# A third neighbour from SBUF, part of a fourth by SyncE, and VectorE's register loads moved: the item stage of a recommender kernel

## Chip, cores and metric

The kernel runs on one core of a Trainium2 chip. The metric is the device time of one execution in microseconds, as a median over runs. One further execution was recorded by the hardware profiler; durations of single instructions come from that one.

## What is computed

There are 50001 items. Each has two embeddings of 32 numbers (E_in, E_out), an embedding of 64 numbers, and 32 neighbours. For each item and each of the two tables, the scores against the 32 neighbours pass through a softmax, and the neighbours' rows are summed with these weights. This makes a table of 128 numbers per item. Then, for 16384 users with a history of 100 items and a target each, rows of that table are fetched, multiplied with the target's row, sent through a layer of 128 units, and weighted.

```python
def _neighbor_attn(E, near_full):
    V = E[near_full]
    scores = jnp.einsum('nd,nkd->nk', E, V) / jnp.sqrt(jnp.float32(GEO_HALF))
    w = jax.nn.softmax(scores, axis=-1)
    return jnp.einsum('nk,nkd->nd', w, V)
...
a_sus = _neighbor_attn(E_in, near_full)
a_inf = _neighbor_attn(E_out, near_full)
hist_bi = jnp.concatenate([a_sus[history], a_inf[history]], axis=-1)
h = jnp.concatenate([E_hist[history], hist_bi], axis=-1)
x = h * t[:, None, :]
z = jax.nn.relu(jnp.einsum('bld,hd->blh', x, W1) + b1)
scores = jnp.einsum('blh,h->bl', z, W2[0])
```

## The kernel before

The kernel has two stages, one after the other. The **item stage** fills the table in DRAM; the **user stage** gathers from it (12800 indirect DMAs at L438, 128 rows each) and is not touched by the change.

The item stage works on blocks of 128 items, one item per partition. NITER x NSUB = 23 x 17 = 391 blocks; `load(it)` (L128 to L163) brings indices, own embeddings and rows for 17 blocks at a time by SyncE. For a block s the tile v holds the 32 neighbours of each of the 128 items, 64 numbers (both tables) per neighbour, so 256 bytes. It is filled in two ways:

- `gather(s)` (L198) issues one indirect DMA per neighbour on GpSimd (L215): 128 rows of 256 bytes, one to each partition. With NAUX = 2 it does so for 30 of the 32 neighbours. A path on which SyncE fetches one neighbour row by row (L206 to L213) stands in the code, but SPNUM = 0 leaves it unused.
- The last NAUX neighbours come out of SBUF. The whole two-table embedding is held transposed in geoT, two items to a column (`transposed`, L165, done once at the start out of 66 loads st at L171). `columns(s, a, i0)` (L222) loads 32 column addresses into registers of one engine (L189) and issues 32 small copies, geoT column to g column (L229). `turn` (L231) transposes g back on TensorE, `even` (L238, ScalarE) and `odd_half` (L245, VectorE, a predicated copy) put the right half of the column into v. AUX says which engine copies which 32 columns: "AAAA" is four groups on ScalarE (A), "DDDD" four on VectorE (D).

After that VectorE multiplies v with the item's own row (prod, L258), sums to scores (L268), takes the largest (L272, L273); ScalarE makes the exponents (L281); VectorE weights the neighbours (L294, once per table), sums (L309) and scales (L310); ScalarE copies the result into the second table's row (`finish`, L317), and every 17 blocks writes both tables.

The order is written out by hand: the stage runs under a manual schedule for TensorE, ScalarE, VectorE and SyncE, so each engine executes in the order of the code. In turn s of the loop at L337, GpSimd gathers block s, block s-1 is scored, block s-2 weighted, block s-3 finished. Eight pieces of work (L343) alternate with the groups of copies for block s (L353 to L359), which are dealt out evenly over the eight. v has five buffers, g two, wv and prod one. DMAs issued by SyncE and ScalarE share eight completion semaphores in rotation, and the next DMA on one waits for the one before.

Of the kernel before, what the change touches and what calls it, by code (L numbers as in the profile page):

```python
# [31 lines left out]
NSUB = 17  # L32
# [2 lines left out]

AUX = ("AAAA", "DDDD",)
NAUX = len(AUX)
SPNUM, SPDEN = 0, 1  # L40
ENGINE = {"A": E.Activation, "D": E.DVE}
NREG = 32
PAIRS = ROWS // 2
# [11 lines left out]
def kernel(  # L55
# [57 lines left out]
    with (  # L113
# [11 lines left out]
        its = {}  # L125
        subs = {}
# [71 lines left out]
        def gather(s):  # L198
            it, j = divmod(s, NSUB)
            nidx = its[it][0]  # L200
            v = n_v.tile([P, K, 2, G], F32, name="v")
            g = [n_g.tile([P, P], F32, name=f"g{a}") for a in range(NAUX)]
            subs[s] = {"v": v, "g": g}
            k1 = K - NAUX - 1
            by_sp = s * SPNUM % SPDEN < SPNUM
            if by_sp:  # L206
                for i0 in range(0, P, NREG):
                    vals = registers(s, 0, E.SP, i0, 0, (ITEMS - 1) * 8 * G)
                    for i in range(NREG):
                        nc.sync.dma_start(  # L210
                            v[i0 + i : i0 + i + 1, k1].rearrange("p t d -> p (t d)").bitcast(U8),
                            egeo_b[:, ds(vals[i], 8 * G)],
                        )  # L213
            for k in range(k1 if by_sp else k1 + 1):
                nc.gpsimd.indirect_dma_start(  # L215
                    out=v[:, k].rearrange("p t d -> p (t d)"),
                    out_offset=None,
                    in_=egeo,
                    in_offset=bass.IndirectOffsetOnAxis(ap=nidx[:, j, k : k + 1], axis=0),
                )  # L220

        def columns(s, a, i0):  # L222

            e = AUX[a][i0 // NREG]
            vals = registers(s, a + 1, ENGINE[e], i0, geoT_at, geoT_at + 4 * (PAIRS - 1))
            g = subs[s]["g"][a].bitcast(U8)
            copy = nc.scalar.copy if e == "A" else nc.vector.tensor_copy
            for i in range(i0, i0 + NREG):
                copy(g[:, 4 * i : 4 * i + 4], geoT_b[:, ds(vals[i - i0] - geoT_at, 4)])  # L229

        def turn(s):  # L231
            back = n_pt.tile([P, 4, P], F32, name="pt")
            for a in range(NAUX):
                nc.tensor.transpose(back[:, a, :], subs[s]["g"][a], ident)  # L234
            subs[s]["back"] = back
            subs[s]["aux"] = subs[s]["v"][:, K - NAUX : K].rearrange("p k t d -> p k (t d)")

        def even(s):  # L238
            it, j = divmod(s, NSUB)
            nc.scalar.copy(subs[s]["aux"], subs[s]["back"][:, 0:NAUX, 0 : 2 * G])  # L240
            own_ps = n_ps.tile([P, 1, 2 * G], F32, name="own_ps")
            nc.scalar.copy(own_ps[:, 0, :], its[it][1][:, j, :])
            subs[s]["own"] = own_ps

        def odd_half(s):  # L245
            it, j = divmod(s, NSUB)
            nc.vector.copy_predicated(
                subs[s]["aux"],
                its[it][4][:, j, :]
                .rearrange("p (a o) -> p a o", o=1)  # L250
                .to_broadcast([P, NAUX, 2 * G]),
                subs[s]["back"][:, 0:NAUX, 2 * G : 4 * G],
            )

        def products(s):
            v = subs[s]["v"]
            prod = n_p.tile([P, K, 2, G], F32, name="prod")
            nc.vector.tensor_tensor(  # L258
                prod.rearrange("p k t d -> p k (t d)"),
                v.rearrange("p k t d -> p k (t d)"),  # L260
                subs[s]["own"].to_broadcast([P, K, 2 * G]),
                ALU.mult,
            )
            subs[s]["prod"] = prod

        def scores(s):
            sc = n_s.tile([P, 2, K], F32, name="sc")
            nc.vector.tensor_reduce(  # L268
                sc.rearrange("p t k -> p k t"), subs[s]["prod"], AX.X, ALU.add
            )  # L270
            top = n_s.tile([P, 2], F32, name="top")
            nc.vector.tensor_reduce(top, sc, AX.X, ALU.max)  # L272
            nc.vector.tensor_scalar(top, top, -scale, None, ALU.mult)  # L273
            subs[s]["sc"] = (sc, top)

        def exponents(s):
            sc, top = subs[s]["sc"]
            ex = n_ps.tile([P, 2, K], F32, name="ex")
            tot = n_s.tile([P, 2, 1], F32, name="tot")
            for t in range(2):  # L280
                nc.scalar.activation(  # L281
                    ex[:, t, :],
                    sc[:, t, :],
                    AF.Exp,
                    bias=top[:, t : t + 1],
                    scale=scale,
                    accum_out=tot[:, t, :],
                )
            subs[s]["ex"] = (ex, tot)

        def weighted(s, t):
            if t == 0:
                subs[s]["wv"] = n_p.tile([P, 2, G, K], F32, name="wv")
            nc.vector.tensor_tensor(  # L294
                subs[s]["wv"][:, t].rearrange("p d k -> p k d"),
                subs[s]["v"][:, :, t, :],
                subs[s]["ex"][0][:, t, :]
                .rearrange("p (k o) -> p k o", o=1)
                .to_broadcast([P, K, G]),
                ALU.mult,  # L300
            )

        def attend(s):
            it, j = divmod(s, NSUB)
            row = its[it][2]
            tot = subs[s]["ex"][1]
            nc.vector.reciprocal(tot, tot)
            att = n_s.tile([P, 2, G], F32, name="att")
            nc.vector.tensor_reduce(att, subs[s]["wv"], AX.X, ALU.add)  # L309
            nc.vector.tensor_tensor(  # L310
                row[:, j, DE:D].rearrange("p (t d) -> p t d", t=2),
                att,
                tot.to_broadcast([P, 2, G]),
                ALU.mult,
            )

        def finish(s):  # L317
            it, j = divmod(s, NSUB)
            _, _, row, trow, _, _ = its[it]
            for t in range(2):  # L320
                nc.scalar.copy(
                    trow[:, j, t * G : (t + 1) * G], row[:, j, D - (t + 1) * G : D - t * G]
                )
            if j == NSUB - 1:
                nc.scalar.dma_start(table_v[it], row)
                nc.scalar.dma_start(ttab_v[it][:, :, DE:D], trow)
                del its[it]
            del subs[s]

        NT = NITER * NSUB  # L330
# [3 lines left out]
        blocks = [(a, i0) for a in range(NAUX) for i0 in range(0, P, NREG)]  # L334
        acts = [(a, i0) for a, i0 in blocks if AUX[a][i0 // NREG] == "A"]
        dves = [(a, i0) for a, i0 in blocks if AUX[a][i0 // NREG] == "D"]
        for s in range(NT + 3):  # L337
            if s < NT:
                if s % NSUB == NSUB // 2 and s // NSUB + 1 < NITER:
                    load(s // NSUB + 1)  # L340
                gather(s)
            one, two, three = (0 <= s - d < NT for d in (1, 2, 3))
            work = [  # L343
                lambda: one and turn(s - 1),
                lambda: (two and weighted(s - 2, 0), one and even(s - 1)),
                lambda: two and weighted(s - 2, 1),
                lambda: one and (odd_half(s - 1), products(s - 1)),
                lambda: one and scores(s - 1),
                lambda: two and attend(s - 2),
                lambda: three and finish(s - 3),  # L350
                lambda: one and exponents(s - 1),
            ]
            for w in range(len(work)):  # L353
                work[w]()
                if s < NT:
                    for blocks in (acts, dves):
                        n = len(blocks)
                        for c in blocks[-(-w * n // 8) : -(-(w + 1) * n // 8)]:
                            columns(s, *c)  # L359


    num = const.tile([P, UC], F32, name="num")
# [8 lines left out]
    with (  # L371
# [125 lines left out]
        for s in range(len(groups) + 2):  # L497
            if s < len(groups):
                c, g = groups[s]
# [12 lines left out]
    with (  # L512
# [12 lines left out]
        s = f_s.tile([P, 1], F32, name="s")  # L525
# [72 lines left out]
```

## Time and profile before

| | |
|---|---|
| median of 3 runs | 30856.08 us (30855.88 to 30856.29) |
| the profiled execution | 30865.45 us, of it 30863.6 us span |
| GpSimd busy | 23284.3 us, 75% |
| VectorE busy | 12128.8 us, 39% |
| ScalarE busy | 7843.2 us, 25% |
| gathers of the item stage (L215) | 11730, 944 ns each |
| gathers of the user stage (L438) | 12800, 944 ns each |
| copies at L229 | 50048 on ScalarE, 50048 on VectorE |
| granted TensorE clock, mean | 0.802 |

In the profile, POOL is GpSimd, DVE is VectorE, ACT is ScalarE, SP is SyncE, PE is TensorE; a q behind the name means that the engine's sequencer issues and the engine itself stays idle. A row of the groups gives the line, the operation, out<-in, the count, then busy time in us and mean ns of one, then the idle time of the engine just before these instructions and what ended it. "issue" is idle time that no recorded event of another engine ended. A row of the waits gives who waited for whom: total us, times, longest. A row of the timeline gives start, duration, and in brackets the idle time before. Loads of registers do not count as busy; they show as idle time of the engine. The small copies at L229 overlap each other, so a group of 32 is much shorter than 32 times the mean.

### The profile page before, as it was taken

To read this page: it belongs to the slowest core of one execution; us is meant where nothing else is said; L and a number is where in the kernel's file an instruction comes from. 1 tells how busy PE (TensorE), PEld (TensorE's weight loads), DVE (VectorE), ACT (ScalarE), POOL (GpSimd) and SP (SyncE) were. 2 spreads that over 40 slices of the span, in tenths; PEclk is the share of its full clock that TensorE was granted. 3 is DMA by queue.
4 is the path that set the end of the run, shared out by engine and by line. 5 is a ranking of instruction groups with operands and counts; after the bars stand their busy time and mean duration, and the time that the engine had idled before them with its cause. 6 is when DMAs were issued, how large, how long until landed. Compare 5 with 4: busy or idle time off the path is not lost.

```text
span 30863.6 us, 246685 instructions
## 1 busy us (share of the span) xinstructions
PE 13340.6 (43%) x45932; PEld 7630.5 (25%) x45932; DVE 12128.8 (39%) x58485; ACT 7843.2 (25%) x56963; POOL 23284.3 (75%) x24664
## 2 busy tenths in 40 slices
PE   0000000000000000000778778877877877887787
PEld 0000000000000000000444444444444544454444
DVE  5555555555555555555222222222222222222222
ACT  4333333333333333333111111111111111111111
POOL 7777777777777777777777777777777777777777
PEclk9999999999999999999665666666566566656656
DMA  2111111111111111111222222222222222222221
GB/s 67 31 31 31 32 34 31 31 31 32 34 31 31 31 35 31 31 31 29 54 53 54 54 53 54 53 53 53 54 53 54 53 54 53 53 53 54 53 54 52
DMA packets 966199, 1351.82 MB, mean 44 GB/s; under 512 B 548416, under 2 KB 561280, under 8 KB 961696
## 3 DMA queue, kind: packets, MB, share of 16 engines
q0 software_dynamic: 789056, 1233.20, 17.1%
q10 hardware_dynamic: 103920, 51.31, 0.6%
q1 hardware_dynamic: 71664, 51.54, 0.6%
q14 instruction: 1192, 9.76, 0.1%
q8 instruction: 367, 6.01, 0.1%
HBM read 1295.95 MB, written 51.30 MB: 44 GB/s over the span
## 4 chain that ended last, share of the span: by engine, by line
POOL 56%; issue 23%; DMA 12%; PE 7%; DVE 1%; another core or an unknown queue 0%; ACT 0%; POOLq 0%; SPq 0%; ACTq 0%; DVEq 0%
POOL v L215 33%; POOL h L438 23%; DMA h<-table,hidx 10%; PE z_ps L473 3%; DMA v<-in_egeo_dram,nidx 2%; PE score L482 2%; PE hT_ps L453 2%; DVE xT L455 1%; DVE hsum L458 0%; DMA st<-in_egeo_dram 0%; PE pt L180 0%; POOL t L400 0%; POOLq L438 0%; ACT g L229 0%
## 5 line engine op out<-in xcount | busy, mean ns | idle before, releaser
L438 POOL DMA_INDIRECT h<-table,hidx x12800 | 12084.6, 944 | 3899.7 <-issue 3451.0
L215 POOL DMA_INDIRECT v<-in_egeo_dram,nidx x11730 | 11078.2, 944 | 3599.4 <-issue 3484.2
L453 PE MATMUL hT_ps<-ident,h 128*128 128x128 f32 x12800 | 5070.5, 414 | 3207.2 <-DMA h<-table,hidx 3025.5
L455 DVE TENSOR_TENSOR xT<-hT_ps,tT 128x1024 f32<-128x1024 f32 (+1 forms) x1664 | 1968.4, 1183 | 10942.7 <-PE hT_ps L453 10942.5
L234 PE MATMUL pt<-ident,g 128*128 128x128 f32 x782 | 363.9, 471 | 13297.0 <-DVE g L229 8118.8
L473 PE MATMUL z_ps<-xT,w1T 128*128 128x512 f32 x6400 | 5799.9, 1007 | 26.6 <-DVE xT L455 26.3
L229 ACT COPY g<-geoT 128x4 uint8 x50048 | 4919.0, 189 | 2153.7 <-issue 2152.4
L474 ACT ACTIVATE z<-z_ps,b_sb 128x512 f32<-128x512 f32 x3200 | 2201.1, 688 | 12756.3 <-PE z_ps L473 12748.7
L229 DVE COPY g<-geoT 128x4 uint8 x50048 | 3885.9, 194 | 2268.1 <-issue 2149.5
L453 PEld LDWEIGHTS hT_ps<-ident,h 128*128 128x128 f32 x12800 | 2439.0, 194 | 8517.2 <-DMA h<-table,hidx 7853.9
L482 PEld LDWEIGHTS score<-w_sb,z 128*128 128x128 f32 x25600 | 4330.9, 255 | 0.6 <-issue 0.5
L482 PE MATMUL score<-w_sb,z 128*128 128x1 f32 x25600 | 4022.1, 279 | 0.1
L234 PEld LDWEIGHTS pt<-ident,g 128*128 128x128 f32 x782 | 141.9, 183 | 13514.9 <-DVE g L229 8226.4
L258 DVE TENSOR_TENSOR prod<-v,own_ps 128x2048 f32<-128x2048 f32 x391 | 894.4, 2287 | 4148.8 <-DMA v<-in_egeo_dram,nidx 4147.6
L458 DVE TENSOR_REDUCE hsum<-h 128x8 f32<-128x1024 f32 (+1 forms) x1664 | 1942.6, 1167 | 0.0
L473 PEld LDWEIGHTS z_ps<-xT,w1T 128*128 128x128 f32 x6400 | 1884.4, 354 | 115.0 <-issue 70.4
L294 DVE TENSOR_TENSOR wv<-v,ex 128x1024 f32<-128x1024 f32 x782 | 1404.3, 1869 | 0.0
L281 ACT ACTIVATE ex<-sc,top 128x32 f32<-128x32 f32 x782 | 227.7, 291 | 4355.4 <-DVE top L273 4342.8
L268 DVE TENSOR_REDUCE sc<-prod 128x64 f32<-128x2048 f32 x391 | 894.5, 2288 | 13.5
L309 DVE TENSOR_REDUCE att<-wv 128x64 f32<-128x2048 f32 x391 | 882.9, 2258 | 0.0
L240 ACT COPY v<-pt 128x128 f32<-128x128 f32 x391 | 104.0, 266 | 2520.2 <-PE pt L234 2520.2
L489 DVE TENSOR_TENSOR ea<-ea,keep 128x100 f32<-128x100 f32 x128 | 33.8, 264 | 1177.1 <-ACT ea L488 1177.1
(67 smaller groups left out, 1536.8 us busy)
## 6 DMA issues: line engine op xcount, KB each, us to landing
h<-table,hidx POOLq DMA_INDIRECT x12800, 2.5
v<-in_egeo_dram,nidx POOLq DMA_INDIRECT x11730, 2.4
table<-row ACTq DMA_DIRECT2D x23, 1088.0 KB, 4.5
own<-in_egeo_dram SPq DMA_DIRECT2D x23, 544.0 KB, 4.0
row<-in_ehist_dram SPq DMA_DIRECT2D x23, 544.0 KB, 6.4
ttab<-trow ACTq DMA_DIRECT2D x23, 544.0 KB, 6.1
ttab<-in_etgt_dram ACTq DMA_DIRECT2D x1, 12500.0 KB, 52.4
st<-in_egeo_dram SPq DMA_DIRECT2D x65, 192.0 KB, 2.4
```

The lines of the kernel that those rows point to most:

```text
L215: nc.gpsimd.indirect_dma_start(out=v[:, k].rearrange("p t d -> p (t d)"), out_offset=None, in_=egeo, in_offset=bass.IndirectOffsetOnAxis(a ...
L229: copy(g[:, 4 * i : 4 * i + 4], geoT_b[:, ds(vals[i - i0] - geoT_at, 4)])
L258: nc.vector.tensor_tensor(prod.rearrange("p k t d -> p k (t d)"), v.rearrange("p k t d -> p k (t d)"), subs[s]["own"].to_broadcast([P, K, ...
L268: nc.vector.tensor_reduce(sc.rearrange("p t k -> p k t"), subs[s]["prod"], AX.X, ALU.add)
L294: nc.vector.tensor_tensor(subs[s]["wv"][:, t].rearrange("p d k -> p k d"), subs[s]["v"][:, :, t, :], subs[s]["ex"][0][:, t, :] .rearrange( ...
L438: nc.gpsimd.indirect_dma_start(out=h[:, q, :], out_offset=None, in_=table, in_offset=bass.IndirectOffsetOnAxis(ap=u["hidx"][:, l : l + 1], ...
L453: nc.tensor.transpose(hT_ps[:, q, :], h[:, q, :], ident)
L455: x = nc.vector.tensor_tensor(xT[:, 0:w, :], hT_ps[:, 0:w, :], u["tT"].to_broadcast([D, w, P]), ALU.mult)
L458: s = nc.vector.tensor_reduce(u["hsum"][:, g * LW : g * LW + w], h[:, 0:w, :], AX.X, ALU.add)
L473: nc.tensor.matmul(z_ps, w1T, xT[:, q : q + LG, :], start=True, stop=True)
L474: nc.scalar.activation(z[:, q : q + LG, :], z_ps, AF.Relu, bias=b1_sb)
L482: nc.tensor.matmul(u["score"][:, l : l + 1], z[:, q, :], w2_sb, start=True, stop=True)
```

## The change

NAUX becomes 3: one neighbour more comes out of SBUF, in twelve groups of 32 copies per block, six on ScalarE and six on VectorE (AUX "AAAA", "AADD", "DDDD"). SPNUM, SPDEN = 2, 3: in the blocks s with 2s mod 3 below 2, SyncE fetches one neighbour more, by four loads of 32 registers and 128 DMAs of one row of 256 bytes (L210); in the others GpSimd still gathers it. The even dealing of the copies over eight pieces is replaced by a written order, in which each group on VectorE but the last stands behind one of its long operations. For this `scores` is cut into `scores` and `largest`, and `attend` into `attend` and `attended`. The exponents of block s-1 come after the weights of block s-2 in the code, the finish of s-3 last.

```diff
-AUX = ("AAAA", "DDDD",)
+AUX = ("AAAA", "AADD", "DDDD",)
-SPNUM, SPDEN = 0, 1
+SPNUM, SPDEN = 2, 3
...
-            work = [
-                lambda: one and turn(s - 1),
-                lambda: (two and weighted(s - 2, 0), one and even(s - 1)),
-                lambda: two and weighted(s - 2, 1),
-                lambda: one and (odd_half(s - 1), products(s - 1)),
-                lambda: one and scores(s - 1),
-                lambda: two and attend(s - 2),
-                lambda: three and finish(s - 3),
-                lambda: one and exponents(s - 1),
-            ]
-            for w in range(len(work)):
-                work[w]()
-                if s < NT:
-                    for blocks in (acts, dves):
-                        n = len(blocks)
-                        for c in blocks[-(-w * n // 8) : -(-(w + 1) * n // 8)]:
-                            columns(s, *c)
+            act(0)
+            for i in range(5, len(dves)):
+                dve(i)
+            if one:
+                turn(s - 1)
+                even(s - 1)
+                odd_half(s - 1)
+                products(s - 1)
+            dve(0)
+            act(1)
+            if one:
+                scores(s - 1)
+            dve(1)
+            act(2)
+            if one:
+                largest(s - 1)
+            if two:
+                weighted(s - 2, 0)
+            dve(2)
+            act(3)
+            if two:
+                weighted(s - 2, 1)
+            dve(3)
+            act(4)
+            if one:
+                exponents(s - 1)
+            if two:
+                attend(s - 2)
+            dve(4)
+            act(5)
+            if two:
+                attended(s - 2)
+            for i in range(6, len(acts)):
+                act(i)
+            if three:
+                finish(s - 3)
```

Here `act(i)` and `dve(i)` call `columns` for block s with the i-th group of ScalarE and of VectorE. `largest` holds the lines of the largest score and its scaling (L272, L273 before), `attended` the last product (L310 before). The SyncE path that is now used is this one, unchanged:

```python
if by_sp:
    for i0 in range(0, P, NREG):
        vals = registers(s, 0, E.SP, i0, 0, (ITEMS - 1) * 8 * G)
        for i in range(NREG):
            nc.sync.dma_start(
                v[i0 + i : i0 + i + 1, k1].rearrange("p t d -> p (t d)").bitcast(U8),
                egeo_b[:, ds(vals[i], 8 * G)],
            )
```

More of the change, by code (lines that the diff above doesn't have):

```diff
@@ L270, in scores, with largest @@
             )
+            subs[s]["sc"] = sc
+        def largest(s):
+            sc = subs[s]["sc"]
             top = n_s.tile([P, 2], F32, name="top")
@@ L303, in attend @@
         def attend(s):
-            it, j = divmod(s, NSUB)
-            row = its[it][2]
             tot = subs[s]["ex"][1]
@@ L309, in attend, with attended @@
             nc.vector.tensor_reduce(att, subs[s]["wv"], AX.X, ALU.add)
+            subs[s]["att"] = att
+        def attended(s):
+            it, j = divmod(s, NSUB)
+            row = its[it][2]
+            att, tot = subs[s]["att"], subs[s]["ex"][1]
             nc.vector.tensor_tensor(
@@ L341, with act, dve @@
                 gather(s)
+            now = s < NT
             one, two, three = (0 <= s - d < NT for d in (1, 2, 3))
-            work = [
-                lambda: one and turn(s - 1),
-                lambda: (two and weighted(s - 2, 0), one and even(s - 1)),
-                lambda: two and weighted(s - 2, 1),
-                lambda: one and (odd_half(s - 1), products(s - 1)),
-                lambda: one and scores(s - 1),
-                lambda: two and attend(s - 2),
-                lambda: three and finish(s - 3),
-                lambda: one and exponents(s - 1),
-            ]
-            for w in range(len(work)):
-                work[w]()
-                if s < NT:
-                    for blocks in (acts, dves):
-                        n = len(blocks)
-                        for c in blocks[-(-w * n // 8) : -(-(w + 1) * n // 8)]:
-                            columns(s, *c)
+            def act(i):
+                if now and i < len(acts):
+                    columns(s, *acts[i])
+            def dve(i):
+                if now and i < len(dves):
+                    columns(s, *dves[i])
+            act(0)
[34 more added lines that the diff above has]
+                finish(s - 3)
     num = const.tile([P, UC], F32, name="num")
```

## The prediction

> **What bounds the kernel now.** I read the page's forty slices first, then the costliest groups, the waits of GpSimd and VectorE over steady item work (1000 to 14000 us), and one item block in the timeline.
>
> ```profile
> POOL 7777777777777777777777777777777777777777
> POOL 56%; issue 23%; DMA 12%; PE 7%; DVE 1%; another core or an unknown queue 0%; ACT 0%; POOLq 0%; SPq 0%; ACTq 0%; DVEq 0%
> L215 POOL DMA_INDIRECT v<-in_egeo_dram,nidx x11730 | 11078.2, 944 | 3599.4 <-issue 3484.2
> ```
>
> GpSimd is evenly seven tenths busy, and its idle time is "issue": 944 ns of gather and 0.30 us before the next, always. In the timeline the start-to-start step is 1.249 us (7000.91, 7002.16, 7003.41 and so on). An item block of 128 rows costs 30 gathers, 37.5 us, and 391 blocks make 11730 x 1.249 = 14651 us, the first half of the run. Nothing else sets that half, as the other engines show:
>
> ```profile
> DVE prod L258 <- DMA v<-in_egeo_dram,nidx: 3795.3, 347, 13.2
> ACT ex L281 <- DVE top L273: 3961.5, 347, 13.5
> POOL v L215 <- DVE wv L294: 19.0, 1, 19.0
> ```
>
> VectorE waits 3795.3/347 = 10.9 us of every 37.5 for the last gather of the block; ScalarE waits 11.4 us behind VectorE and 6.5 us more before L240 (2245.9 us, 347 times). GpSimd waited for another engine once, 19.0 us, at the start. So a gather removed is worth its full 1.249 us until VectorE, ScalarE or SyncE takes longer than the shortened block.
>
> ```profile
> 7037.27 2.29 DVE L258 TENSOR_TENSOR prod<-v,own_ps 128x2048 f32<-128x2048 f32 x1 [10.79 <-DMA v<-in_egeo_dram,nidx]
> 7039.59 2.29 DVE L268 TENSOR_REDUCE sc<-prod 128x64 f32<-128x2048 f32 x1
> 7041.91 0.22 DVE L272 TENSOR_REDUCE top<-sc 128x2 f32<-128x64 f32 x1
> 7042.16 0.17 DVE L273 TENSOR_SCALAR top<-top 128x2 f32<-128x2 f32 x1
> 7044.37 2.47 DVE L229 COPY g<-geoT 128x4 uint8 x32 [2.04 <-issue]
> ...
> 7057.65 3.60 DVE L294 TENSOR_TENSOR wv<-v,ex 128x1024 f32<-128x1024 f32 x2
> 7061.10 2.34 DVE L229 COPY g<-geoT 128x4 uint8 x32
> ```
>
> The 2.04 us "issue" before the first 32 copies is the load of their 32 registers, with nothing running behind it; behind the 3.60 us pair at L294 the same load shows no gap.
>
> **GpSimd's gathers.** NAUX goes from 2 to 3 and SyncE takes one more neighbour in the blocks where 2s mod 3 is below 2, which is 261 of 391. GpSimd issues 261 x 28 + 130 x 29 = 11078 gathers in place of 11730: 652 fewer, 652 x 1.249 = 814 us. The mean block becomes 35.4 us. All of it is on the path, if the others stay below 35.4.
>
> **VectorE.** It goes from 4 to 6 groups of 32 copies. Per block: 6 x 2.4 (L229 rows, 2.34 to 2.70) = 14.4; prod 2.29, sc 2.29, weights 2 x 1.87, att 2.26 = 10.6; top, its scaling, reciprocal and the last product 0.8; the predicated copy grows from 128 to 192 columns, 0.28 to about 0.35. Register loads: five of six now stand behind an operation of 1.87 to 2.29 us and also begin while the last copies before them are still running (two groups back to back show 1.1 to 1.6 us of gap, not 2.04), so they cost nothing; the sixth, behind the 0.23 us product, about 1.4. Sum 27.6 us. Cover: the wait for the gathers, 35.4 - 27.6 = 7.8 us. Without any hidden load it would be 27.6 + 5 x 2.05 = 37.9 and bind.
>
> **ScalarE.** 6 groups: 3.14 us of copies and a 0.9 us gap when the groups follow each other (7023.51 to 7027.77 is 4.2 us), so 25; exponents about 1.0, even and own 0.5, the two row copies 0.3. Sum 27 us, also covered. Its exponents wait for the largest score, which VectorE has about 10 us after prod; ScalarE gets there after four groups, 17 us, so that wait goes. PE has one transpose more (0.47 us), nothing beside 35. Neither can go below nothing in cost or bring a gain while GpSimd is the bound.
>
> **SyncE.** This is the open part. In 261 blocks it issues 4 register loads and 128 single-row copies of 256 bytes, each addressed by a register. Before has no such copy, so I bound the step from issue to issue.
>
> ```profile
> 0.75 0.39 SPq L91 DMA_DIRECT2D b_sb<-in_b_dram  x1
> 1.19 0.42 SPq L93 DMA_DIRECT2D w_sb<-in_w_dram  x1
> 7037.06 0.34 SPq L130 DMA_DIRECT2D nidx<-in_near_dram  x1
> 7037.49 0.38 SPq L132 DMA_DIRECT2D own<-in_egeo_dram  x1
> ```
>
> The shortest record, 0.33 to 0.34, and the 0.05 us between neighbours give 0.38 us for a 128-row copy: the high end by the trace. [...] The low end is what landings allow: in the program as built each of these copies waits for the one eight before it, and small SyncE transfers land in 1.6 to 2.0 us, so 2.0/8 = 0.25 us.
>
> A block of SyncE is T = 128c + 4 x 2.05. [...] SyncE runs ahead of GpSimd (five v buffers; it waits for the block five back, which VectorE frees some three blocks early), so what counts is its total, 170 us (the end of its st loads) + 261 T, against the end of GpSimd's gathers: 8.6 + 13838 + the start's stall, 13922. It stays hidden up to T = 52.7, c = 0.348. It equals the old 14679 at T = 55.6, c = 0.371. [...] The loads for the next iteration (three at L130 to L134) stand in the same queue behind a block's copies; they are needed nine blocks later and before waited for table writes anyway, so nothing.
>
> **The start.** SyncE can't gather for block 0 before the st loads end at 170 us, so v of block 0 is whole at 170 + 47 = 217. GpSimd has issued five blocks by 8.6 + 142 x 1.249 = 186 and waits for block 0's buffer, freed in the next turn but one: 217 + 28 (a VectorE turn) + 17 (to the second weight) = 262. Stall 76 us, where before had 19: +57. [...]
>
> **Sum.** Span 30863.6 - 814 + 57 = 30107. The profiled execution took 30865.45, 9.4 more than the median of the runs (30856.08); by the median: 30856 - 757 = 30099, about 30100. The user half (12800 gathers at L438) and the 24 us between the halves are left as they are.
>
> **Rivals.**
> 1. SyncE becomes the bound and the kernel is slower. Place: SyncE's queue at L210; price 261 x 128 = 33408 us per us of c; it decides from c = 0.371. At c = 0.40, T = 59.4: 170 + 261 x 59.4 = 15673 in place of 14679, 31850 us. [...] For it: the 0.38 of the rows. Against: those copies had 128 rows.
> 2. SyncE binds but below the old block, c from 0.348 to 0.371: 30100 to 30856. At 0.36, T = 54.3: 170 + 14172 = 14342, 30519 us.
> 3. VectorE binds since loads are not hidden: 37.9 x 391 = 14819 in place of 14651, and the start: about 31080. Against: the L294 pair hides the load already.
> 4. The gathers' step grows from SyncE's traffic. The stretch with SyncE's first loads has the same 1.249, so I give it nothing of its own.
>
> **Chances.** GpSimd still binds, 30070 to 30160: 0.63. Rival 2: 0.11. Rival 1: 0.22. Rival 3: 0.04. The range reaches from 30060 up through rival 2 and the near part of rivals 1 and 3, to 31200 (T to 57, about 0.06 of the 0.26); the rest, 0.2, is left out above. The likeliest case's own range is 30070 to 30160. A measurement here can tell about 0.2% (62 us) from no change: faster 0.73, within 0.03, slower 0.24.
>
> **What would show it.** L215 x11078, still 944 ns with 0.30 before it; prod waiting for v about 7 to 8 us a block; five of six groups of VectorE copies without an issue gap; the one long wait of GpSimd at the start near 76 us; SyncE's copies at L210 about 0.30 us apart, SyncE waiting for v buffers. It is wrong if GpSimd waits for wv in every block, and prod waits for v<-in_egeo_dram of SyncE: then c is above 0.348. If VectorE has no wait left before prod, rival 3 holds.

## The result, and the profile after

The median fell from 30856.19 to 30160.73 us: ratio 0.9774, 95% interval 0.9759 to 0.979, 695 us saved where 757 were forecast. The profiled execution took 30160.56 us, of it 30158.8 span. In two of the four groups of runs below the kernel before itself took 40327 and 40521 us, and the times of such a group are compared only with each other.

From the page after, the rows that answer to those shown of before:

```profile
POOL 6777777777777777777777777777777777777777
POOL 36%; issue 18%; DMA 16%; SPq 15%; PE 6%; DVE 4%; DVEq 0%; POOLq 0%; ACT 0%; ACTq 0%
L215 POOL DMA_INDIRECT v<-in_egeo_dram,nidx x11078 | 10458.2, 944 | 3515.2 <-issue 3221.9
L258 DVE TENSOR_TENSOR prod<-v,own_ps 128x2048 f32<-128x2048 f32 x391 | 894.8, 2288 | 2684.3 <-DMA v<-in_egeo_dram 1470.5
```

The gathers are 11078 as counted, still 944 ns each, and the timeline still has 1.25 us from one to the next, so SyncE's traffic does not slow them (the prediction's rival 4). VectorE's idle time before prod fell from 4148.8/391 = 10.6 us a block in the page of before to 2684.3/391 = 6.9. The new sight is SyncE's queue with 15% in the chain of work that ended last: the chain now runs through SyncE's copies for part of the item stage, so SyncE is close to the bound, although GpSimd is just as busy as before.

In the waits of GpSimd over the whole run, the rows above a few us that are not "issue" are few:

```profile
POOL v L215 <- DMA v<-in_egeo_dram: 163.3, 286, 76.4
POOL v L215 <- DVE wv L298: 53.4, 2, 46.1
POOL t L437 <- DMA ttab<-trow: 26.9, 1, 26.9
```

Three long stalls are in the item stage, and the timeline of GpSimd has them at these places:

```profile
262.55 0.94 POOL L215 DMA_INDIRECT v<-in_egeo_dram,nidx  x1 [76.35 <-DMA v<-in_egeo_dram]
...
339.48 0.94 POOL L215 DMA_INDIRECT v<-in_egeo_dram,nidx  x1 [7.22 <-DVE wv L298]
...
952.61 0.94 POOL L215 DMA_INDIRECT v<-in_egeo_dram,nidx  x1 [46.13 <-DVE wv L298]
```

The span's difference comes out of them: gathers -814; start 76.4 in place of 19.0, +57; 339 us, +7; 952 us, +46; the boundary between the stages 26.9 in place of 23.5, +3; the rest, about -4, is not placed. Sum -705; the spans differ by 704.8. From the last item gather to the end both took 16184 us.

One block of VectorE after, from the timeline:

```profile
7040.86 2.29 DVE L258 TENSOR_TENSOR prod<-v,own_ps 128x2048 f32<-128x2048 f32 x1 [5.85 <-DMA v<-in_egeo_dram]
7043.08 2.42 DVE L229 COPY g<-geoT 128x4 uint8 x32
7045.42 2.27 DVE L268 TENSOR_REDUCE sc<-prod 128x64 f32<-128x2048 f32 x1
7047.61 2.57 DVE L229 COPY g<-geoT 128x4 uint8 x32
...
7052.46 2.70 DVE L229 COPY g<-geoT 128x4 uint8 x32 [0.26 <-issue]
...
7064.98 2.66 DVE L229 COPY g<-geoT 128x4 uint8 x32 [1.28 <-issue]
7067.37 0.36 DVE L247 COPY_PREDICATED v<-odd,pt 128x192 f32<-128x192 int32 x1
7075.41 2.29 DVE L258 TENSOR_TENSOR prod<-v,own_ps 128x2048 f32<-128x2048 f32 x1 [7.68 <-DMA v<-in_egeo_dram]
```

Behind prod and sc the copies start without a gap, behind the first weight after 0.26 us, and the last group shows 1.28 us. From one prod to the next are 34.6 us, of them 7.7 waiting: VectorE needs 26.9.

### The profile page after: what moved, and what is told of

Its sections match the earlier page's. It is cut to its first block, busy times and chain, and to the rows that moved or that the text cites. A ratio compares the mean times of both kernels' runs of the same rounds, so it can differ in the third digit from the quotient of the medians.

```text
span 30158.8 us, 370867 instructions
## 1 busy us (share of the span) xinstructions
PE 13513.8 (45%) x46323; PEld 7666.4 (25%) x46323; DVE 13913.7 (46%) x83509; ACT 10305.2 (34%) x81987; POOL 22658.7 (75%) x24012
## 4 chain that ended last, share of the span: by engine, by line
POOL 36%; issue 18%; DMA 16%; SPq 15%; PE 6%; DVE 4%; DVEq 0%; POOLq 0%; ACT 0%; ACTq 0%
POOL h L475 24%; DMA h<-table,hidx 13%; SPq L210 12%; POOL v L215 12%; PE z_ps L510 3%; SPq L189 3%; DMA v<-in_egeo_dram,nidx 2%; DVE g L229 1%; PE score L519 1%; PE hT_ps L490 1%; DVE xT L492 1%; DVE sc L268 0%; DVE prod L258 0%; DVEq L189 0%; DMA v<-in_egeo_dram 0%
## 5 line engine op out<-in xcount | busy, mean ns | idle before, releaser
L215 POOL DMA_INDIRECT v<-in_egeo_dram,nidx x11078 | 10458.2, 944 | 3515.2 <-issue 3221.9
L229 ACT COPY g<-geoT 128x4 uint8 x75072 | 7377.3, 189 | 3385.9 <-issue 2729.6
L229 DVE COPY g<-geoT 128x4 uint8 x75072 | 5877.5, 197 | 808.2 <-issue 688.4
L234 PE MATMUL pt<-ident,g 128*128 128x128 f32 x1173 | 543.7, 471 | 12496.1 <-ACT g L229 10195.4
L234 PEld LDWEIGHTS pt<-ident,g 128*128 128x128 f32 x1173 | 213.3, 184 | 12822.0 <-ACT g L229 10467.5
L258 DVE TENSOR_TENSOR prod<-v,own_ps 128x2048 f32<-128x2048 f32 x391 | 894.8, 2288 | 2684.3 <-DMA v<-in_egeo_dram 1470.5
L285 ACT ACTIVATE ex<-sc,top 128x32 f32<-128x32 f32 x782 | 227.0, 290 | 1343.5 <-DVE top L277 1330.8
L240 ACT COPY v<-pt 128x192 f32<-128x192 f32 x391 | 123.8, 317 | 1135.4 <-PE pt L234 1135.4
```

Source lines behind the costliest of these rows:

```text
L215: nc.gpsimd.indirect_dma_start(out=v[:, k].rearrange("p t d -> p (t d)"), out_offset=None, in_=egeo, in_offset=bass.IndirectOffsetOnAxis(a ...
```

## The experiments

My theory: the item stage lasts as long as GpSimd's gathers; the work of SyncE, VectorE and ScalarE fits beside them and costs nothing; what the sum lacked are stalls early in the stage. The rivals: placing the register loads is what lets VectorE keep up; SyncE runs without a bound of its own; the 46 us stall is SyncE's lateness alone.

### Four kernels, where the kernel before takes 40327 us

The four are the columns alone, the whole change in the old order, the new order alone, SyncE's copies alone. Edits, each against the kernel it names:

```diff
 e1, against after:
-SPNUM, SPDEN = 2, 3
+SPNUM, SPDEN = 0, 1
 e2, against before (so the old dealing of the copies stays):
-AUX = ("AAAA", "DDDD",)
+AUX = ("AAAA", "AADD", "DDDD",)
-SPNUM, SPDEN = 0, 1
+SPNUM, SPDEN = 2, 3
 e6, against after:
-AUX = ("AAAA", "AADD", "DDDD",)
-SPNUM, SPDEN = 2, 3
+AUX = ("AAAA", "DDDD",)
+SPNUM, SPDEN = 0, 1
 e7, against before:
-SPNUM, SPDEN = 0, 1
+SPNUM, SPDEN = 2, 3
```

> The change without SyncE's copies (three columns, new order, GpSimd gathers 29 neighbours in every block). If GpSimd's gathers alone set the item stage: 391 gathers fewer than before, 391 x 1.249 = 488 us, and the start's stall grows from 19 to about 60 us since VectorE's and ScalarE's columns of block 0 take longer and the new order weights block 0 later: 30856 - 488 + 41 = 30410. No GpSimd wait near 950 us. If VectorE's or ScalarE's copies were the bound, the block would be longer than 29 x 1.249 = 36.2 us and the time above 30500.

> Three columns and SyncE in two of three blocks, but the old even dealing of the copies in place of the new order. If GpSimd is the bound and the register loads are hidden anyway by the wait for the gathers: VectorE needs about 33 us of a 35.4 us block (27.6 less the 1.4, and about 6.9 us of exposed loads), so no change: 30160, or 20 us less since the old order frees block 0's buffer earlier, say 30140. If placing the loads is what makes the change work, VectorE's block is above 35.4 us: at 38 us, 391 x 2.6 = 1000 us more, 31150, with no wait before prod.

> The new order alone (two columns, no SyncE copies, 30 gathers). If GpSimd is the bound: no change but a stall at the start of about 33 us in place of 19, 30870, and VectorE's wait for the gathers grows from 10.9 to about 14 us a block. If the loads' placement had been worth something by itself, it would be faster than 30800.

> SyncE's copies alone on the kernel before (two columns, old order). If SyncE's 50.9 us of work in two of three blocks is hidden: 261 gathers fewer, 326 us, a stall at the start of about 48 us in place of 19, and 0 to 46 us behind the first table write: 30560 to 30600. If SyncE's traffic slows the gathers or VectorE, the step of 1.249 us grows: each 0.01 us on 11469 gathers is 115 us more.

The kernel before took 40327.38 us beside them. Ratios to it: e1 1.0546 (1.0528 to 1.0563), e2 1.1281 (1.1262 to 1.13), e6 0.9875 (0.9859 to 0.9892), e7 1.1305 (1.1287 to 1.1324). The expectations are for a kernel before of 30856 us and can't be judged from these. In the timeline of the columns alone (e1), all engines:

```profile
7035.25 0.19 ACT L229 COPY g<-geoT 128x4 uint8 x1 [0.51 <-issue]
7035.87 0.94 POOL L215 DMA_INDIRECT v<-in_egeo_dram,nidx  x1 [0.30 <-issue]
7035.95 0.17 DVE L229 COPY g<-geoT 128x4 uint8 x1 [1.23 <-issue]
7037.12 0.94 POOL L215 DMA_INDIRECT v<-in_egeo_dram,nidx  x1 [0.30 <-issue]
7037.34 0.19 ACT L229 COPY g<-geoT 128x4 uint8 x1 [1.90 <-issue]
7037.35 0.17 DVE L229 COPY g<-geoT 128x4 uint8 x1 [1.23 <-issue]
```

A copy takes what it takes elsewhere (0.17 and 0.19 us), but the copies start at multiples of 0.70 us (7035.25, 7035.95, 7037.35), mostly one at a time for VectorE and ScalarE, where 32 of them took 2.4 and 3.1 us before; GpSimd's gathers keep 1.25 us in this window. So it is not the copies that are slow but their succession, and in long stretches. What holds them up isn't known.

The order alone and SyncE's copies alone were run again on another chip, and there the kernel before took 40521.05 us:

> The new order alone (two columns, no SyncE copies), as e6 but on another chip. GpSimd as the bound: 30870, no change but some 14 us at the start, and VectorE's wait for the gathers grows from 10.9 to about 14 us a block. If VectorE's hidden loads are worth time by themselves: below 30800.

> SyncE's copies alone on the kernel before (two columns, old order), as e7 but on another chip. SyncE hidden: 261 gathers fewer, 326 us, about 30 us more at the start and 0 to 46 us at the first table write: 30560 to 30600. If SyncE's traffic slows the gathers by 0.01 us each: 30680 and more.

r7 took 40004.63 us, ratio 0.9875 (0.9858 to 0.9891), r8 45858.25 us, ratio 1.1316 (1.1297 to 1.1335): the ratios of e6 and e7 over again. The order alone and SyncE alone thus have no number where the kernel before takes 30856 us; what they do there follows only from differences between other kernels, below.

### The columns alone, and the old order, where the kernel before takes 30855 us

The kernels are those of e1 and e2.

> The same kernel as e1 (three columns, new order, no SyncE copies) on another chip, since in the first call the kernel before itself took 40327 us. If the kernel before is near 30856 again: GpSimd's gathers as the bound give 30856 - 488 + 41 = 30410, with a stall of about 60 us at the start and no GpSimd wait near 950 us; copies on VectorE or ScalarE as the bound give above 30500.

> The same kernel as e2 (three columns, SyncE in two of three blocks, old even dealing) on another chip. If the register loads are hidden by the wait for the gathers wherever they stand: VectorE needs about 33 us of 35.4, and the time is 30140 to 30160. If placing them is what makes the change work: VectorE's block is above 35.4 us, 38 us would give 31150.

The kernel before took 30854.55 us. r1 took 30408.13 us, ratio 0.9855 (0.9839 to 0.9872): the forecast to 2 us. Three columns are worth 446 us without SyncE, and GpSimd is the bound: it waits for another engine once for long, 55.5 us at the start. From r1 to after it is 247 us, SyncE's part. Its 261 gathers are worth 326; the longer stall at the start (21) and those at 339 and 952 us (7 and 46) take some 74 of it back.

r2 took 30134.79 us, ratio 0.9767 (0.9751 to 0.9783): 26 us less than after. So the new order of the copies does not carry the change; it costs a little, 14 of the 26 us in a longer stall at the start (76.4 against 62.2). VectorE in r2, from the timeline:

```profile
7016.95 2.29 DVE L258 TENSOR_TENSOR prod<-v,own_ps 128x2048 f32<-128x2048 f32 x1
...
7024.06 2.39 DVE L229 COPY g<-geoT 128x4 uint8 x32 [2.04 <-issue]
...
7030.94 2.44 DVE L229 COPY g<-geoT 128x4 uint8 x32 [1.98 <-issue]
7034.70 2.73 DVE L229 COPY g<-geoT 128x4 uint8 x32 [1.33 <-issue]
7038.52 2.66 DVE L229 COPY g<-geoT 128x4 uint8 x32 [1.09 <-issue]
...
7051.56 2.29 DVE L258 TENSOR_TENSOR prod<-v,own_ps 128x2048 f32<-128x2048 f32 x1 [2.12 <-DMA v<-in_egeo_dram,nidx]
```

The loads show as gaps of 1.1 to 2.0 us, 6.4 us a block, and what they add comes out of the wait before prod, which shrinks to 2.1 us. 34.6 less 2.1 is 32.5 us of need in a block of 35.4. The exposed loads cost nothing because VectorE isn't the bound; by estimate, with some 3 us more need (35.4 less 32.5) they would.

### SyncE pushed over its edge

```diff
-SPNUM, SPDEN = 2, 3
+SPNUM, SPDEN = 3, 4
```

> SyncE in 294 of 391 blocks in place of 261, new order. If SyncE's 50.9 us a block (128 copies at 0.320 and 4 loads at 2.2, from the profile of after) hides only while its sum is below GpSimd's: SyncE ends at 171 + 294 x 50.9 = 15136 and becomes the bound, 27 us to the user stage and 16157 us after it: 31320, up to 31460 if each table write holds SyncE's queue for some 6 us. GpSimd then waits for wv in most blocks. If SyncE runs beside without a bound of its own: 33 gathers fewer than after, 30160 - 41 = 30120.

It took 31571.01 us, ratio to before 1.0227 (1.021 to 1.0244): slower than the kernel before, although GpSimd issues 32 gathers fewer than after. GpSimd's waits, and the longest of VectorE's between 500 and 13000 us:

```profile
POOL v L215 <- DVE wv L298: 1498.8, 122, 22.8
POOL v L215 <- DMA v<-in_egeo_dram: 150.2, 230, 80.3
POOL t L437 <- DMA ttab<-trow: 109.3, 1, 109.3
DVE prod L258 <- DMA v<-in_egeo_dram: 1818.2, 96, 25.2
```

GpSimd stands still 122 times because VectorE frees v late, and VectorE is late because SyncE's rows are; SyncE itself waits for others only 15 us in that window. After its last gather GpSimd stands 109 us more. SyncE's copies run from 174 to 15430 us for 293 blocks (the expectation said 294): 52.1 us a block and not 50.9, so SyncE ends 294 us later than expected, and the time lies 110 us above the expected range. (50.9 is the time from block to block early in after; the two terms that the expectation names for it make only 128 x 0.320 + 4 x 2.2 = 49.8.) The rival, SyncE without a bound of its own (30120), falls.

At the same 52.1 us a block, after has 261 x 52.1 = 13598 us of work in the 13745 us from SyncE's first to its last copy. The bound of SyncE was 1% away.

### The stall at 952 us

At the first table write of after, ScalarE in the timeline, and the SyncE copy that stands last before it:

```profile
857.35 0.33 ACT L329 COPY trow<-row 128x32 f32<-128x32 f32 x2
924.10 0.34 ACTq L333 DMA_DIRECT2D table<-row  x1
928.47 0.61 ACTq L334 DMA_DIRECT2D ttab<-trow  x1
```

```profile
922.89 0.23 SPq L210 DMA_DIRECT2D v<-in_egeo_dram  x1
```

ScalarE is done at 857.7 and issues its write at 924.1: the trace records the same completion semaphore (106) for this write and for the copy that SyncE issued 1.2 us before, the last on that semaphore in SyncE's newest block. It is so at each of the 22 writes of after that stand before SyncE's last copy: the table write starts 1.2 to 1.7 us after a SyncE copy with the same semaphore. For 66 us ScalarE, and behind it VectorE's predicated copy (67.25 us of wait in the timeline), stand still. To take that away without touching SyncE, the two writes were moved to GpSimd, whose DMAs don't stand in that rotation (in the trace of after they record the semaphores 109 to 116, those of SyncE and ScalarE 100 and 102 to 108):

```diff
-                nc.scalar.dma_start(table_v[it], row)
-                nc.scalar.dma_start(ttab_v[it][:, :, DE:D], trow)
+                nc.gpsimd.dma_start(table_v[it], row)
+                nc.gpsimd.dma_start(ttab_v[it][:, :, DE:D], trow)
```

> As after, but the two table writes every 17 blocks are issued by GpSimd and not by ScalarE, so that they don't share completion semaphores with SyncE's copies. If the 46 us wait of GpSimd near 950 us comes from ScalarE waiting at its first table write for SyncE's last copies of the newest block: that wait is gone, ScalarE has no wait of tens of us for ttab, and the 46 writes cost GpSimd about 1.25 us each: 30160 - 46 + 57 = 30171. If the 46 us comes from SyncE's being late by itself: it stays, 30217.

It took 30159.34 us, ratio 0.9774 (0.9757 to 0.979). Between 342 us and its last item gather, GpSimd is nowhere more than 2.6 us from one gather to the next; the first pair of writes shows in its timeline as

```profile
872.47 0.61 POOL L333 DMA_DIRECT2D table<-row  x1
898.08 1.34 POOL L334 DMA_DIRECT2D ttab<-trow  x1
```

so 1.9 us a pair, and 42 us for the 22 pairs that stand among gathers: what the stall gave back, the writes took. ScalarE's wait for ttab is gone from its list. SyncE begins as late here as in after (78.7 us of stall at the start). So it takes the shared semaphore to make the 46 us, and SyncE's lateness by itself doesn't make them.

### SyncE off in the first six blocks, in both orders

```diff
-            by_sp = s * SPNUM % SPDEN < SPNUM
+            by_sp = s >= 6 and s * SPNUM % SPDEN < SPNUM
```

> As after, but SyncE fetches nothing in blocks 0 to 5 (four gathers more on GpSimd). If the stalls at the start come from SyncE's beginning at 171 us and running behind: the start's stall falls to that of the columns alone (56 us in place of 76), those at 339 and 950 us go: 30160 + 5 - 20 - 7 - 46 = 30092, and ScalarE's waits for ttab go. If they don't come from there: 30165.

> The old even dealing, three columns, SyncE in two of three blocks from block 6 on. If the two findings add (order worth nothing or 20 us at the start, late SyncE removes the stalls): 30135 + 5 - 43 - 3, and some 15 us less at the start: 30080. If the old order leaves VectorE too little room (33 us of 35.4), it is at or above r5.

r5 took 30092.6 us (ratio 0.9752, 0.9736 to 0.9768), as forecast: 68 us less than after for four gathers more. r6, the same edit on r2, took 30074.83 us (ratio 0.9746, 0.973 to 0.9763). It is the fastest of all kernels here, 86 us below after. GpSimd's only long stall of the item stage in r5 and in r6:

```profile
246.58 0.94 POOL L215 DMA_INDIRECT v<-in_egeo_dram,nidx  x1 [56.31 <-DVE wv L298]
```

```profile
233.00 0.94 POOL L215 DMA_INDIRECT v<-in_egeo_dram,nidx  x1 [43.13 <-DVE wv L294]
```

One thing of my expectation failed: ScalarE's waits for ttab did not go. In r5 they are 490.8 us in 21 times, the longest 71.4. GpSimd doesn't feel them. In after, too, only the first of them reaches it: the second is longer (81.0 against 75.2 us, the two writes included) and stalls nothing. So the 46 us take both, the shared semaphore and SyncE's rows being late at that moment; that the five v buffers cover such a stop as soon as the rows are in time is the likely reason, and not shown by itself.

With before (19.0), r1 (55.5), r2 (62.2) and after (76.4) the stall at the start comes apart: 24 us from more columns for block 0 (19.0 to 43.1), 13 from the new order (43.1 to 56.3), 20 from SyncE's late begin (56.3 to 76.4, and 43.1 to 62.2 in the old order).

## Why the prediction was right, point by point

- **GpSimd as the bound, 1.249 us a gather.** Right: 11078 gathers, 944 ns, and r1 came within 2 us of its expectation, which rests on this step.
- **VectorE's 27.6 us.** Measured 26.9 in the block shown. It is covered in both orders. The prediction's bound for loads in the open (37.9) was too high for the old order: there only 6.4 us are exposed, not 10, since the weights still hide two loads, and the need is 32.5. Rival 3 was therefore further away than said.
- **ScalarE.** Groups of 32 come every 4.07 us, as summed. That its wait for the largest score goes was wrong: 1330.8 us of it remain, 3.4 a block, and the likely reason is that VectorE's prod, from which the scores come, itself waits for the gathers. It costs nothing while GpSimd is the bound.
- **SyncE's step.** The mis-sized term. I took c = 0.30 us a copy and 2.05 us a load, so T = 46.6 us a block. A stretch of after in the timeline:

```profile
6999.79 5.34 SPq L210 DMA_DIRECT2D v<-in_egeo_dram  x17
```

Seventeen copies in 5.34 us are 0.32 each: the trace has 0.225 for the copy and, before it, a register move that I had not counted, 0.03 and two gaps. The loads took 2.2. With the rest of a block (the loads for the next iteration, waits, not taken apart further), r3 gives 52.1. No run shows the c = 0.30 behind the 47 us in the sum, nor the T made of it: it was an estimate of mine nearer the low end of 0.25, and the runs showed 0.32 us a copy in after and 52.1 us a block in r3 in their place. The threshold of the prediction was 52.7. So SyncE stayed hidden by 0.6 us a block, where the prediction had counted on 6.1: that it stayed hidden at all was in part luck. With T = 46.6 SyncE would have had some 13745 - 261 x 46.6 = 1580 us to spare and waited for v buffers; it waited for them 233 us. On the two ends: the record of a one-row copy is shorter than that of a 128-row copy (0.225 us in after, 0.33 in before), but not by so much that the landing of eight copies in flight would set the pace: the step stayed at 0.32. The semaphore was free again 1.2 us after the copy's start in the case shown, so that end was 1.2/8 = 0.15, not 0.25.
- **The start, +57.** The size was right to 1 us, partly by luck. The path was the one foreseen, SyncE's last row of block 0 and then VectorE to its second weight; but prod starts at 221 us and not at 217, and from there it takes 41 us and not 45, and the two errors cancel. And the +57 was put on SyncE's begin at 170 us, where without SyncE the stall is already 56: only 20 us are SyncE's; 37 come from the columns and the new order, whose later weights free block 0's buffer later.
- **The table writes, not named at all.** This is where 46 of the missing 62 us were lost. I had noted that the DMAs of SyncE and ScalarE share eight semaphores (100 and 102 to 108 in the trace), and used it only for SyncE's own pace. I had not asked what the rotation does to the other engine: the one that issues two DMAs in 17 blocks waits behind the one that issues 128 in a block. The 7 us at 339 us are not the writes', since r4 keeps them; r5 loses them, so they belong to SyncE's late begin, which the true step makes up by about 1 us a block (35.4 x 1.5 - 52.1) and not by the 6.5 that T = 46.6 would give. The remaining 9 us are no event in the trace: the profiled execution lay 9.4 us above the median before and 0.2 below it after.

## What to carry to other kernels

Where one engine sets the pace, count the instructions taken from it and divide the rest of the work so that each other engine's sum stays below the new block; hiding a stall on an engine that waits anyway was worth nothing here, and cost 26 us. When many small DMAs are put on a queue, look at who shares their completion semaphores: here a rare, large DMA of another engine waited for the newest small one, 66 us at the first table write of after. Time an engine's step from issue to issue with everything that stands between, register moves too, before choosing a share such as 2 in 3; here 3 in 4 turns a gain of 2.3% into a loss of 2.3%.

## What had not been expected of the hardware

A single-row DMA with its address in a register cost SyncE 0.32 us from issue to issue in after. The same programs also ran 31% slower (before, 40327 us) to 51% slower (r2's kernel, 45522 against 30135 us), with the small copies of VectorE and ScalarE starting on a grid of 0.70 us in long stretches (the timelines of e1, e6, r7 and r8); there the change's parts rank the other way round, the new order alone gaining 1.25%, the columns with it losing 5.5% and SyncE's copies alone 13%. It is not the chip alone: r3 to r6, beside which the kernel before took 30859 us, and r7 and r8, beside which it took 40521, ran on the same chip by the record. What it is stays open.
